# Absolute differences on half an image of one sample at a time, its rows quantised one sample ahead and loaded one unit ahead

## The chip, the cores and the metric

The kernel runs on one core of a Trainium2 chip. The metric is the device time of one execution in microseconds. Executions of a kernel agreed within 0.4% here, so runs are compared directly. Experiments run beside the kernel before on the same chip. Ratios are computed as the mean time of one kernel's runs over that of the other's of the same rounds, so they are not quite the ratio of the medians quoted beside them.

## The reference

Four layers, each added to its input after a group norm: a recurrence along the diagonals of the image, an "adder" convolution, a spectral layer, and a small convolutional encoder and decoder. The change concerns the second layer. On 16 samples of 32 channels of 128x128 it quantises the normalised input to integers of -127 to 127 and takes, in place of products, absolute differences:

```python
def _adder2d(qx, qw):      # out[n,f,i,j] = -sum_{c,kh,kw} |patch - w|
    ...
    def per_out(wk):
        return -jnp.sum(jnp.abs(pr - wk[None, :, None]), axis=1)
    out = jax.lax.map(jax.checkpoint(per_out), wf)
    ...
x = x + _L1_conv_ref(_gn(x), L1_conv_weight)
```

Both kernels use |q - w| = 2 max(q - w, 0) - q + w. VectorE or ScalarE computes max(q - w, 0) for one tap of a filter, in f16. TensorE sums it over the channels with a matrix of constants. The sums of q ("the sums" below) are matmuls on the quantised rows themselves, and the sum of w is one constant per filter.

## The kernel before

A unit is 32 rows of four samples, with 32 channels x 4 samples on the 128 partitions. There are 16 units. All eight accumulators (PSUM banks) belong to the current unit. A unit's quantised rows are made in SBUF from rows loaded in f32; nothing goes back to memory but the result.

```python
for g in range(NG):
    for ch in range(H // R):                                     # R = 32
        xc = xp.tile([128, R + 2, W], F32, name="xc")
        nc.sync.dma_start(xc[:, off : off + n, :], cb_view(x1, g, lo, n))
        ...                                                      # quantise into qa (padded rows), qb
        acc = [ps.tile([128, 512], F32, name="acc") for _ in range(8)]
        for tap in range(9):                                     # the sums: 288 matmuls
            for k in range(8):
                for j in range(4):
                    nc.tensor.matmul(acc[k][32 * j : 32 * j + 32, :], sel16[:, 8, :],
                                     window(tap)[:, 4 * k : 4 * k + 4, :], start=tap == 0, stop=False)
        for f8 in range(8):
            for tap in range(9):                                 # 288 tiles of 4096 per partition
                for j in range(4):
                    ...                                          # j == 3: ScalarE, else VectorE
                ...                                              # 32 matmuls on the four tiles
        for k in range(8):                                       # the finish
            v = xc[:, 1 + 4 * k : 5 + 4 * k, :].rearrange("p r w -> p (r w)")
            nc.vector.scalar_tensor_tensor(v, acc[k], sumw, v, ALU.subtract, ALU.add)
            nc.vector.bn_stats(stat[:, g, 8 * ch + k, :], v)
        nc.scalar.dma_start(cb_view(x2, g, R * ch, R), xc[:, 1 : R + 1, :])
```

The transfers of a unit address memory as `[[HW, C], [CHW, 4], [1, n]]`: the slowest dimension is the 32 channels.

Of the kernel before, what the change touches and what calls it, by code (L numbers as in the profile page):

```python
# [6 lines left out]
F32 = mybir.dt.float32  # L7
F16 = mybir.dt.float16
# [7 lines left out]
HW = H * W  # L16
CHW = C * HW
NG = 4
# [20 lines left out]
def cb_view(t, g, row0, nrows):  # L39

    return bass.AP(t.tensor, t.offset + g * 4 * CHW + row0 * W, [[HW, C], [CHW, 4], [1, nrows * W]])


# [28 lines left out]
def norm_stats(nc, pool, ps, mv, n, avg, eps):  # L72



    mean = pool.tile([128, n], F32, name="ns_mean")
    nc.vector.tensor_copy(mean, mv[:, :, 0])
    p1 = ps.tile([128, 512], F32, name="ps")
    nc.tensor.matmul(p1[:, :n], avg, mean, start=True, stop=True)
    m = pool.tile([128, n], F32, name="ns_m")  # L80
    nc.vector.tensor_copy(m, p1[:, :n])
    d = pool.tile([128, n], F32, name="ns_d")
    nc.vector.tensor_sub(d, mean, m)
    nc.vector.tensor_mul(d, d, d)
    nc.vector.tensor_add(d, d, mv[:, :, 1])
    p2 = ps.tile([128, 512], F32, name="ps")
    nc.tensor.matmul(p2[:, :n], avg, d, start=True, stop=True)
    v = pool.tile([128, n], F32, name="ns_v")
    nc.vector.tensor_copy(v, p2[:, :n])
    return m, inv_sqrt(nc, pool, v, n, eps)  # L90
# [10 lines left out]
def stage0(nc, tc, keep, cst, x, w0, b1, b2, x1):  # L101
# [3 lines left out]
    with ExitStack() as ctx:  # L105
# [104 lines left out]
        with tc.tile_pool(name="s0_ps2", bufs=2, space=PSUM) as ps:  # L210
            out = []
            for v in norm_stats(nc, sm, ps, mv, NG, cst["avg2_bc"], 1e-5):
                p = ps.tile([128, 512], F32, name="ps")
                nc.tensor.matmul(p[:, :NG], cst["bc_to_cb"], v, start=True, stop=True)
                out.append(keep.tile([128, NG], F32, name=f"s0_out{len(out)}"))
                nc.vector.tensor_copy(out[-1], p[:, :NG])
            return out


def stage1(nc, tc, keep, cst, sel16, m1, r1, x1, w, x2):  # L220
# [4 lines left out]
    R = 32  # L225
    with ExitStack() as ctx:
        sm = ctx.enter_context(tc.tile_pool(name="s1_sm", bufs=1))
        r128 = sm.tile([128, NG], F32, name="r128")
        nc.vector.tensor_scalar(r128, r1, 128.0, None, ALU.mult)


        qw = sm.tile([128, 288], F32, name="qw")
        nc.sync.dma_start(qw, bass.AP(w.tensor, w.offset, [[288, 32], [0, 4], [1, 288]]))
        top = sm.tile([128, 1], F32, name="top")
        nc.vector.tensor_reduce(top, qw, AX.X, ALU.max, apply_absolute_value=True)
        alltop = sm.tile([128, 1], F32, name="alltop")
        nc.gpsimd.partition_all_reduce(alltop, top, 128, bass_isa.ReduceOp.max)
        scale = sm.tile([128, 1], F32, name="scale")
        nc.vector.tensor_scalar(scale, alltop, 1.0 / 127.0, 1e-8, ALU.mult, ALU.max)
        nc.vector.tensor_scalar(scale, scale, 2.0**0.5, None, ALU.mult)  # L240
        nc.vector.tensor_scalar(scale.bitcast(I32), scale.bitcast(I32), 0x7F800000, None, ALU.bitwise_and)
        nc.vector.reciprocal(scale, scale)
        nc.vector.tensor_scalar(qw, qw, scale, -127.0, ALU.mult, ALU.max)
        nc.vector.tensor_scalar(qw, qw, 127.0, RND, ALU.min, ALU.add)
        nc.vector.tensor_scalar(qw, qw, RND, None, ALU.subtract)
        neg = sm.tile([128, 288], F32, name="neg")
        nc.vector.tensor_scalar(neg, qw, -1.0, None, ALU.mult)


        taps = sm.tile([128, 32], F32, name="taps")  # L250
        nc.vector.tensor_reduce(taps, qw.rearrange("p (f t) -> p f t", t=9), AX.X, ALU.add)
        tapb = sm.tile([128, 32, 4], F32, name="tapb")
        nc.vector.tensor_tensor(tapb, bcast(taps[:, :], 2, 4), bcast(cst["m4_cb"], 1, 32), ALU.mult)
        sumw = sm.tile([128, 1], F32, name="sumw")
        with tc.tile_pool(name="s1_ps0", bufs=1, space=PSUM) as ps:
            p = ps.tile([128, 512], F32, name="ps")
            nc.tensor.matmul(p[:, :1], tapb.rearrange("p f b -> p (f b)"), cst["ones"][:, :1], start=True, stop=True)
            nc.vector.tensor_scalar(sumw, p[:, :1], 2.0**-7, None, ALU.mult)

        stat = sm.tile([128, NG, 32, 6], F32, name="stat2")  # L260
        xp = ctx.enter_context(tc.tile_pool(name="s1_x", bufs=2))
        tp = ctx.enter_context(tc.tile_pool(name="s1_t", bufs=1))
        qp = ctx.enter_context(tc.tile_pool(name="s1_q", bufs=2))
        dp = ctx.enter_context(tc.tile_pool(name="s1_d", bufs=2))
        with tc.tile_pool(name="s1_ps", bufs=8, space=PSUM) as ps:
            for g in range(NG):
                for ch in range(H // R):
                    lo, hi = max(R * ch - 1, 0), min(R * ch + R + 1, H)
                    off = lo - (R * ch - 1)
                    n = hi - lo  # L270
                    xc = xp.tile([128, R + 2, W], F32, name="xc")
                    nc.sync.dma_start(xc[:, off : off + n, :], cb_view(x1, g, lo, n))


                    qa = qp.tile([128, R + 2, W + 2], F16, name="qa")
                    qb = qp.tile([128, R + 2, W], F16, name="qb")
                    t = tp.tile([128, R + 2, W], F32, name="t")
                    tv, qv = t[:, off : off + n, :], qb[:, off : off + n, :]
                    nc.vector.tensor_scalar(
                        tv, xc[:, off : off + n, :], m1[:, g : g + 1], r128[:, g : g + 1], ALU.subtract, ALU.mult  # L280
                    )
                    nc.vector.tensor_scalar(tv, tv, -127.0, 127.0, ALU.max, ALU.min)
                    nc.vector.tensor_scalar(qv, tv, RND, RND, ALU.add, ALU.subtract)
                    nc.scalar.copy(qa[:, off : off + n, 1 : W + 1], qv)
                    nc.gpsimd.memset(qa[:, :, 0], 0.0)
                    nc.gpsimd.memset(qa[:, :, W + 1], 0.0)
                    for edge, row in ((ch == 0, 0), (ch == H // R - 1, R + 1)):
                        if edge:
                            nc.gpsimd.memset(qa[:, row, :], 0.0)
                            nc.gpsimd.memset(qb[:, row, :], 0.0)  # L290

                    def window(tap):
                        kh, kw = tap // 3, tap % 3
                        return qb[:, kh : kh + R, :] if kw == 1 else qa[:, kh : kh + R, kw : kw + W]

                    acc = [ps.tile([128, 512], F32, name="acc") for _ in range(8)]
                    for tap in range(9):
                        for k in range(8):
                            for j in range(4):
                                nc.tensor.matmul(  # L300
                                    acc[k][32 * j : 32 * j + 32, :],
                                    sel16[:, 8, :],
                                    window(tap)[:, 4 * k : 4 * k + 4, :],
                                    start=tap == 0,
                                    stop=False,
                                )
                    for f8 in range(8):
                        for tap in range(9):
                            ds = []
                            for j in range(4):  # L310
                                i = 9 * (8 * j + f8) + tap
                                if j == 3:
                                    d = dp.tile([128, R, W], F16, name="d_act", bufs=2)
                                    nc.scalar.activation(d, window(tap), AF.Relu, bias=neg[:, i : i + 1])  # L314
                                else:
                                    d = dp.tile([128, R, W], F16, name="d_dve", bufs=6)
                                    nc.vector.tensor_scalar(  # L317
                                        d, window(tap), qw[:, i : i + 1], 0.0, ALU.subtract, ALU.max
                                    )
                                ds.append(d)  # L320
                            for k in range(8):
                                for j in range(4):
                                    nc.tensor.matmul(  # L323
                                        acc[k][32 * j : 32 * j + 32, :],
                                        sel16[:, f8, :],
                                        ds[j][:, 4 * k : 4 * k + 4, :],
                                        start=False,
                                        stop=f8 == 7 and tap == 8,
                                    )
                    for k in range(8):  # L330
# [830 lines left out]
```

## Time and profile before

| | us |
|---|---|
| median of 3 executions | 9256.16 |
| stage, first VectorE tile to end of the last finish | 4524.4 (1432.0 to 5956.4) |
| unit to unit | 283.4 |
| VectorE tile / ScalarE tile, start to start | 1.196 / 3.60 |

The prediction below shows the slices, the chain and the groups. One view it does not show is worth having first: a stretch in which two loads of 2.1 MB ran (columns: the stretch, its length, busy time and instructions of each engine, the granted clock, the mean busy share of the 16 DMA engines, GB/s).

```profile
core 0: us, PE busy (x) PEld busy (x) DVE busy (x) ACT busy (x) POOL busy (x), PEclk, DMA share, GB/s
1412.00:1418.00 6.00, 0.26 (x2) 0.29 (x2) 3.03 (x11) 0.00 (x0) 0.71 (x3) 0.50 0.99 358
```

A share of 0.99 means that these loads used all 16 engines: in the packet records, 16 of their rows move at once in most of this stretch. The 8.32 us of the first of them is the figure that the prediction took for the changed kernel's transfers.

### The profile page before, as it was taken

What the parts mean: (1) busy time and instruction counts of PE and PEld (TensorE: products, weight loads), DVE (VectorE), ACT (ScalarE), POOL (GpSimd) and SP (SyncE); (2) the same over time, 40 slices, a digit from 0 to 9 for tenths busy, and PEclk for the clock granted to TensorE, in tenths of its full rate; (3) what the DMA queues carried; (4) which work ended last, traced back from release to release, by engine and by line L of the source; (5) the groups of instructions that cost most, each with busy time, mean ns of one, the idle gap of its engine ahead of it and who ended that gap; (6) DMA issues with size and microseconds to landing.
All of it is one profiled execution on the core that took longest, in us unless ns stands there. A gap on an engine that the chain in (4) does not pass through costs nothing.

```text
span 9251.5 us, 253991 instructions
## 1 busy us (share of the span) xinstructions
PE 7875.1 (85%) x117746; PEld 5052.1 (55%) x117746; DVE 6114.6 (66%) x7543; ACT 5084.6 (55%) x3270; POOL 332.4 (4%) x529
## 2 busy tenths in 40 slices
PE   4999988999999999999999999794845968768955
PEld 3888874445444444544445544493734645545832
DVE  5444448999999999999999999830634233232233
ACT  1444437989989899998989989700000110101122
POOL 0111110000000000000000000000000000000000
PEclk9999998999999999999999999855555968778977
DMA  9799921000000000000000000242731111111067
GB/s 199 57 80 78 73 28 30 20 20 20 1 20 20 20 20 12 10 20 20 20 20 1 20 20 10 74 126 54 253 107 53 42 57 36 52 42 36 26 161 182
DMA packets 1503138, 494.74 MB, mean 53 GB/s; under 512 B 1416956, under 2 KB 1420540, under 8 KB 1486332
## 3 DMA queue, kind: packets, MB, share of 16 engines
q1 hardware_dynamic: 1460764, 365.54, 24.5%
q10 hardware_dynamic: 41312, 112.95, 3.7%
q8 instruction: 922, 15.11, 0.7%
q14 instruction: 140, 1.15, 0.0%
HBM read 331.12 MB, written 147.33 MB: 52 GB/s over the span
## 4 chain that ended last, share of the span: by engine, by line
DVE 41%; PE 38%; issue 15%; DMA 2%; SPq 2%; ACT 1%; DVEq 0%; ACTq 0%; POOL 0%; POOLq 0%
DVE d_dve L317 35%; PE acc L905 10%; PE pg L179 5%; PE pg L180 4%; PE acc L646 4%; PE acc L565 3%; PE pg L181 2%; PE acc L300 2%; PE p L379 2%; PE acc L793 2%; PE pf L479 1%; DVE xc L332 1%; PE acc L323 1%; DVE stat L333 1%; PE pa L459 1%
## 5 line engine op out<-in xcount | busy, mean ns | idle before, releaser
L323 PE MATMUL acc<-d_dve,sel 128*32 128x512 f16 x27648 | 3994.7, 379 | 43.7 <-DVE d_dve L317 43.3
L323 PEld LDWEIGHTS <-sel 128*32 128x32 f16 x36864 | 2057.5, 95 | 2042.1 <-issue 217.6
L314 ACT ACTIVATE d_act<-qa,neg 128x4096 f16<-128x4096 f16 x768 | 2803.3, 3697 | 131.4 <-PE acc L323 130.3
L317 DVE TENSOR_SCALAR d_dve<-qa,qw 128x4096 f16<-128x4096 f16 x2304 | 2788.5, 1279 | 110.6 <-PE acc L323 86.0
L323 PE MATMUL acc<-d_act,sel 128*32 128x512 f16 x9216 | 2181.2, 380 | 0.0
L314 ACT ACTIVATE d_act<-qb,neg 128x4096 f16<-128x4096 f16 x384 | 1419.4, 3696 | 0.0
L317 DVE TENSOR_SCALAR d_dve<-qb,qw 128x4096 f16<-128x4096 f16 x1152 | 1409.5, 1279 | 0.0
L905 PE MATMUL acc<-xp,fo_all 32*32 32x512 f32 x25600 | 934.9, 625 | 55.4 <-DVE pooled L806 48.8
L905 PEld LDWEIGHTS acc<-xp,fo_all 32*32 32x32 f32 x25600 | 658.4, 105 | 321.6 <-issue 161.6
L179 PE MATMUL pg<-h,bd 128*128 128x256 f32 x2048 | 652.2, 401 | 58.7 <-DVE h L199 58.4
L190 ACT ACTIVATE gt<-pg,bias 128x256 f32<-128x256 f32 x1024 | 400.9, 474 | 546.0 <-PE pg L181 545.8
L180 PE MATMUL pg<-h,bd 128*128 128x256 f32 x2048 | 622.8, 386 | 0.0
L817 ACT ACTIVATE y<-pooled,fo_b 32x128 f32<-32x128 f32 x256 | 102.4, 400 | 843.6 <-DVE pooled L806 840.2
L646 PE MATMUL acc<-xp 32*32 32x108 f32 x16384 | 326.1, 376 | 233.4 <-issue 228.3
L933 DVE TENSOR_TENSOR acc<-acc,cut 128x4 f32<-128x4 f32 x256 | 28.8, 166 | 700.4 <-PE acc L905 699.3
L181 PE MATMUL pg<-xn,bd 128*128 128x2 f32 (+62 forms) x2048 | 425.8, 289 | 9.4 <-DVE xn L163 9.4
L181 PEld LDWEIGHTS pg<-xn,bd 128*128 128x128 f32 x2048 | 396.6, 194 | 66.4 <-DVE xn L163 10.2
L180 PEld LDWEIGHTS pg<-h,bd 128*128 128x128 f32 x2048 | 398.2, 194 | 56.9
L646 PEld LDWEIGHTS acc<-xp 32*32 32x32 f32 x16384 | 257.3, 135 | 302.4 <-issue 282.6
L617 DVE TENSOR_SCALAR xp<-xp,stats 128x2560 f32<-128x2560 f32 (+1 forms) x64 | 101.0, 1579 | 461.5 <-DMA xp<-x_d 461.4
L194 DVE TENSOR_TENSOR c<-c,gt 128x256 f32<-128x256 f32 x256 | 108.4, 424 | 450.0 <-ACT gt L190 450.0
L179 PEld LDWEIGHTS pg<-h,bd 128*128 128x128 f32 x2048 | 341.4, 195 | 65.6 <-issue 50.0
(233 smaller groups left out, 5197.9 us busy)
## 6 DMA issues: line engine op xcount, KB each, us to landing
xr<-x_d SPq DMA_DIRECT2D x64, 1024.0 KB
xp<-x_d SPq DMA_DIRECT2D x48, 1280.0 KB
x_in<-in_x_dram SPq DMA_DIRECT2D x16, 2048.0 KB
res<-in_x_dram SPq DMA_DIRECT2D x32, 1024.0 KB
x_d<-res SPq DMA_DIRECT2D x32, 1024.0 KB
x_d<-xc ACTq DMA_DIRECT2D x16, 2048.0 KB
x_d<-xr ACTq DMA_DIRECT2D x32, 1024.0 KB
out_dram<-xr ACTq DMA_DIRECT2D x32, 1024.0 KB
```

The source lines that it names most:

```text
L179: nc.tensor.matmul(pg[:, q], wmat(0, q), h_in[:, :, 1:], start=True, stop=False)
L180: nc.tensor.matmul(pg[:, q], wmat(1, q), h_in[:, :, :H], start=False, stop=False)
L181: nc.tensor.matmul(pg[:, q, :, : t + 1], wmat(2, q), xn[:, 2 * c : 2 * c + 2, j, : t + 1], start=False, stop=True,)
L190: nc.scalar.activation(gt[:, q], pg[:, q], AF.Tanh if q == 3 else AF.Sigmoid, bias=bias[:, q : q + 1])
L300: nc.tensor.matmul(acc[k][32 * j : 32 * j + 32, :], sel16[:, 8, :], window(tap)[:, 4 * k : 4 * k + 4, :], start=tap == 0, stop=False,)
L314: nc.scalar.activation(d, window(tap), AF.Relu, bias=neg[:, i : i + 1])
L317: nc.vector.tensor_scalar(d, window(tap), qw[:, i : i + 1], 0.0, ALU.subtract, ALU.max)
L323: nc.tensor.matmul(acc[k][32 * j : 32 * j + 32, :], sel16[:, f8, :], ds[j][:, 4 * k : 4 * k + 4, :], start=False, stop=f8 == 7 and tap == 8,)
L379: nc.tensor.matmul(p1[:, i, :], xh[:, 16 * half + i, :], cst["cas"], start=True, stop=True)
L565: nc.tensor.matmul(acc[blk][32 * j : 32 * j + 32, : rows * n], self.w[part, par, tap, :], src[part, top : top + rows, left : left + n], st ...
L646: nc.tensor.matmul(gram[blk][32 * j : 32 * j + 32, at : at + 36 * n], xp[rows, l, 2 + 32 * j : 34 + 32 * j], xp[rows, l : l + n, 32 * j : ...
L905: nc.tensor.matmul(acc[blk][32 * j : 32 * j + 32, :], wf["all"][rows, tap, :], xp[rows, 4 * j + kh : 4 * j + kh + 4, kw : kw + W], start=t ...
```

## The change

Its intent: larger tiles (8192 or 8320 per partition, so half as many instructions), half an image of one sample per unit (64 rows, 32 units), and two sets of four accumulators, so that a unit's finish and the next unit's matmuls no longer wait for each other. The partitions hold four copies of the 32 channels, and a tile serves four filters. To have the copies, the quantised rows go to memory (`q_d`) and are loaded back four times over. Quantising is done one sample ahead, this load one unit ahead. Cut to its core:

```diff
+def jc_rows(t, b, half, n=16 * W):
+    return bass.AP(t.tensor, t.offset + b * CHW + half * 64 * W, [[16 * W, 4], [HW, C], [1, n]])
 ...
+        def quantise(b, half):
+            t = xp.tile([128, 16 * W], F32, name="xq")                    # 2 buffers
+            nc.sync.dma_start(t, jc_rows(x1, b, half))
+            nc.scalar.activation(t, t, AF.Identity, bias=shift[:, b : b + 1], scale=r128[:, b : b + 1])
+            ...                                                          # two VectorE passes into qt
+            nc.sync.dma_start(bass.AP(q_d.tensor, first, [[16 * P, 4], [(H + 2) * P, C], [1, 16 * P]]), flat)
+        def loaded(b, half):
+            q = qp.tile([128, R + 2, P], F16, name="q")                   # 2 buffers
+            nc.sync.dma_start(q, bass.AP(q_d.tensor, first, [[0, 4], [(H + 2) * P, C], [1, (R + 2) * P]]))
+            xr = rp.tile([128, 16 * W], F32, name="xr1")                  # 2 buffers
+            nc.sync.dma_start(xr, jc_rows(x1, b, half))
+            return q, xr
 ...
+                q, xr = following
+                if (b, half) != (B - 1, 1):
+                    following = loaded(b + half, 1 - half)
+                acc = [ps.tile([128, 512], F32, name="acc") for _ in range(4)]
+                ...                                                      # the sums: 144 matmuls, 32x32 tiles
+                for i in range(72):
+                    act = i % 4 == 3
+                    d = dp.tile([128, R, P], F16, name="d_act" if act else "d_dve", bufs=2 if act else 4)
+                    ...                                                  # one tile, then its 16 matmuls
+                    if i == 7 and before:
+                        finish(*before)                                  # ends with the store of xr to x2
+                    if i in (10, 30) and half == 0 and b + 1 < B:
+                        quantise(b + 1, int(i == 30))
```

Statistics and constants are laid out to match, and the other layers keep their work.

## The prediction

> **What bounds the kernel now.** I read first the slices, to place the stage that the change rewrites:
>
> ```profile
> PE   4999988999999999999999999794845968768955
> DVE  5444448999999999999999999830634233232233
> ACT  1444437989989899998989989700000110101122
> PEclk9999998999999999999999999855555968778977
> DMA  9799921000000000000000000242731111111067
> ```
>
> Slices 7 to 26 (231 us each) are the absolute-difference stage. PE, VectorE and ScalarE all show nine tenths there, DMA nothing. So the limit is one of three engines, or their coupling. The chain of waits, by line, decides between them:
>
> ```profile
> DVE d_dve L317 35%; PE acc L905 10%; PE pg L179 5%; PE pg L180 4%; PE acc L646 4%; PE acc L565 3%; PE pg L181 2%; PE acc L300 2%; PE p L379 2%; PE acc L793 2%; PE pf L479 1%; DVE xc L332 1%; PE acc L323 1%; DVE stat L333 1%; PE pa L459 1%
> ```
>
> VectorE's difference tiles carry 35% of the span, the matmuls that consume them (L323) 1%. PE only looks full[...]. Next the costliest groups:
>
> ```profile
> L323 PE MATMUL acc<-d_dve,sel 128*32 128x512 f16 x27648 | 3994.7, 379 | 43.7 <-DVE d_dve L317 43.3
> L314 ACT ACTIVATE d_act<-qa,neg 128x4096 f16<-128x4096 f16 x768 | 2803.3, 3697 | 131.4 <-PE acc L323 130.3
> L317 DVE TENSOR_SCALAR d_dve<-qa,qw 128x4096 f16<-128x4096 f16 x2304 | 2788.5, 1279 | 110.6 <-PE acc L323 86.0
> L317 DVE TENSOR_SCALAR d_dve<-qb,qw 128x4096 f16<-128x4096 f16 x1152 | 1409.5, 1279 | 0.0
> ```
>
> VectorE idles 110.6 us before its 3,456 tiles, ScalarE 131.4 us before its 1,152: in 4.5 ms both are saturated. A tile's recorded duration (1279 ns) is not its price, because neighbours overlap. The price is start to start, from the timeline early in a unit (unit: one pass of the loop, 16 in all):
>
> ```profile
> 2018.02 7.26 DVE L317 TENSOR_SCALAR d_dve<-qa,qw 128x4096 f16<-128x4096 f16 x6 [3.25 <-PE acc L323]
> 2025.20 3.67 DVE L317 TENSOR_SCALAR d_dve<-qb,qw 128x4096 f16<-128x4096 f16 x3
> 2028.79 7.26 DVE L317 TENSOR_SCALAR d_dve<-qa,qw 128x4096 f16<-128x4096 f16 x6
> ...
> 2018.42 7.31 ACT L314 ACTIVATE d_act<-qa,neg 128x4096 f16<-128x4096 f16 x2
> 2025.63 3.69 ACT L314 ACTIVATE d_act<-qb,neg 128x4096 f16<-128x4096 f16 x1
> 2029.23 7.30 ACT L314 ACTIVATE d_act<-qa,neg 128x4096 f16<-128x4096 f16 x2
> ```
>
> Nine VectorE tiles in 10.77 us: 1.196 us each. Three ScalarE tiles in 10.81 us: 3.60 us. A set of four tiles (three and one) takes 3.59 us on either engine, so the split is balanced to a hundredth. What comes on top is at the unit's edge:
>
> ```profile
> 2272.78 1.40 DVE L332 SCALAR_TENSOR_TENSOR xc<-acc,sumw,xc 128x512 f32<-128x512 f32 x2
> 2274.10 1.27 DVE L333 BATCH_NORM_STATS2 stat<-xc 128x6 f32<-128x512 f32 x2
> 2281.72 0.53 ACTq L334 DMA_DIRECT2D x_d<-xc  x1
> 2293.21 7.31 ACT L314 ACTIVATE d_act<-qa,neg 128x4096 f16<-128x4096 f16 x2 [15.45 <-PE acc L323]
> 2300.43 3.69 ACT L314 ACTIVATE d_act<-qb,neg 128x4096 f16<-128x4096 f16 x1
> ```
>
> The finish (eight pairs of L332 and L333) runs 2272.78 to 2282.80, 10.0 us; ScalarE stands 15.45 us meanwhile. Unit spacing from the chain in order of time: L300 pieces begin at 1430.80 and, fourteen units on, at 5398.88, so 283.4 us. The sum agrees: 216 tiles x 1.196 = 258.3, finish 10.0, quantising 2.52 + 2.39 + 2.4 = 7.3, idle 110.6/16 = 6.9; together 282.5.
>
> [...] Tiles read from `qa`, whose rows lie 130 apart, cost the same 1279 ns as those from `qb`, which are contiguous; a padded output is not shown. [...] in the timeline one column's matmuls come every 0.21 us, so 53.6 ns each.
>
> **The change, part by part.** The arithmetic stays: 16 units of 288 tiles of 4096 become 32 units of 72 tiles of 8192. Four copies of the 32 channels fill the partitions, so one tile serves four filters of one sample. Every fourth tile still goes to ScalarE. I cost one new unit.
>
> (1) VectorE tiles: 54. [...] those with kw = 1 compute all 130 columns[...], a third of them. Mean 2274, so 122.8 us. Two units: 245.6 against 258.3.
>
> (2) ScalarE tiles: 18, [...] mean 7049: 126.9 us. The gain is half the fixed parts; the padding takes a little back.
>
> (3) Finish: four pairs in place of eight per unit, 5.0 us, the same total. But it moves to tile 7 of the next unit, and with 4 accumulators of 8 per unit PE can start the next one at once. Before, all eight banks were held, PE waited, and ScalarE stood 15.45 us.
>
> (4) Quantising: before, three f32 passes, 7.3 us of VectorE per unit, and a copy on ScalarE of about 3.8 (not in its 72 tiles). After, twice per sample: [...] Per sample 3.7 and 4.0.
>
> (5) Matmuls: per tile 16 x 53.6 ns = 0.86 us, while a tile arrives every 1.82 (131/72). The sum of the quantised rows: 288 matmuls took about 18 us (18.29 on the chain for 259); now 144 per unit on 32x32 tiles, at most 144 x 53.6 = 7.7 us. Four VectorE buffers hold 9.1 us of work, which covers that.
>
> (6) DMA: a 2.2 MB load per unit, which four copies of the channels cost, and 0.5 MB out per half. A 2.1 MB load took 8.32 us before; a unit is 131 us long. Hidden. At the start the rows now go to DRAM and back before the first tile: about 6 us more.
>
> Sum per sample: VectorE 245.6 + 10.0 + 3.7 = 259.3; ScalarE 253.8 + 4.0 = 257.8. Against 283.4. VectorE is the bound, ScalarE nearly so. For coupling I allow 3 us a sample: VectorE's finish puts it 5 us behind, ScalarE can be a bit under one 7 us tile ahead (two buffers), and regains 0.23 us per set, so most is absorbed. That is a judgement. Stage: 16 x 259.3 = 4149 + 48 = 4197, against 4524 from the first VectorE tile (1432.0) to the end of the finish (5956.4). Less 327, plus 6: a gain of 321, so **8935 us**. The later stages and the recurrence keep their instructions.
>
> **Rivals.** (A) No absorption: every lump on VectorE and ScalarE is exposed, because PE takes tiles in order and the buffers are short. Then a sample is 253.8 + 4.0 + 10.0 + 3.7 = 271.5, gain 16 x 11.9 = 190: about 9066. For it: two buffers of 7 us on ScalarE, and before the 15.45 us wait at each edge. Against: that wait came from held banks, which are now free.
> (B) A DMA takes the place of the wait: the residual rows `xr1` have two buffers but three units in flight, so that load waits for the store after the finish; if the quantiser's load queued behind it, ScalarE and VectorE would stand perhaps 15 us a sample (an estimate from 8.32 us for 2.1 MB, three transfers of 1 MB). That is 240 us back, about 9175. For it: one queue. Against: in the trace quantising of a unit runs one unit ahead of its place in the source (its first pass at 2007.49, just after the previous unit began at 1998), so order follows readiness.
> (C) [...] a tile becomes 4.4 us and the kernel about 3.5 ms slower. Against: equal times for `qa` and `qb`[...].
> (D) PE becomes the bound: even at half clock 1.72 us per tile are under 1.82; little effect expected.
>
> **Range and chances.** No coupling loss at all gives 8887; a small error in the fixed parts (10 ns on 54 x 32 tiles is 17 us) could take it to 8860. Half to two thirds of rival A's loss gives about 9050. So 8860 to 9050. "Faster by over 2%" means under 9071: A alone just reaches it, B and C miss. I give 0.87 faster, 0.10 within 2%, 0.03 slower (C).
>
> **What would show it.** Right: VectorE tiles 2.26 us start to start, ScalarE 7.01, units 131 us apart, VectorE's idle time in the stage under 60 us, PE's waits now for d tiles after nearly each of them, and ScalarE's 15 us gaps gone. Wrong: VectorE waiting for PE where PE waits for ScalarE's tile (A); waits for DMA loads or by the quantiser ahead of VectorE and ScalarE (B); L317's successor at 4.4 us (C); the sum matmuls on the chain for more than 9 us per unit (D).

The prices of the tiles and passes in parts (1), (2) and (4), and rival C's 4.4 us, are estimates of mine: in the trace of the kernel before, all difference tiles have one size, 4096.

## The result, and the profile after

| | before | after |
|---|---|---|
| median, us | 9252.76 (4 runs: the three above and one more) | 9769.06 (4 runs) |
| ratio, 95% interval | 1 | 1.0557 (1.0538 to 1.0575) |
| first VectorE tile of the stage at, us | 1432.0 | 1509.4 |
| stage to the end of the last finish, us | 4524.4 | 4976.0 (1509.4 to 6485.4) |
| VectorE idle before its tiles, us | 110.6 | 849.9 |

The kernel became 5.6% slower, where 3.5% faster was forecast. The slices of the kernel after show how:

```profile
PE   4999963555545554545454555668565776869965
DVE  5444426889878887878787978972253323332233
ACT  1444326889877887879787978950000010101122
DMA  9899831111111111110111111034462111111157
```

In the stage (slices 7 to 27) VectorE and ScalarE no longer stand at nine, but mostly at seven and eight tenths in turn. No engine is full any more, so something is waited for. The chain of waits by line, in the kernel after:

```profile
PE acc L946 9%; DMA q<-q_d 9%; ACT d_act L357 8%; PE pg L174 4%; PE pg L175 4%; DMA x_d<-xr 4%; PE acc L687 3%; DMA xq<-x_d 3%; DVE d_dve L359 3%; PE pg L176 2%; PE acc L606 2%; PE p L420 2%; PE acc L834 1%; PE pf L520 1%; PE acc L364 1%
```

Three transfers of the stage, absent before, now carry about 15% of the span (8.5, 3.6 and 3.2% before rounding): the load of the quantised rows, the store of the result, and the load for the quantiser. The costliest groups after:

```profile
L359 DVE TENSOR_SCALAR d_dve<-q,qw 128x8192 f16<-128x8192 f16 (+1 forms) x1728 | 3940.9, 2359 | 849.9 <-PE acc L364 826.6
L357 ACT ACTIVATE d_act<-q,neg 128x8192 f16<-128x8192 f16 (+1 forms) x576 | 4066.6, 7148 | 602.9 <-PE acc L364 578.0
L341 PE MATMUL acc<-q,sel 32*32 32x512 f16 x4608 | 149.2, 504 | 841.8 <-DMA q<-q_d 841.8
```

Read them from the bottom. PE stands 841.8 us before the sums (L341), waiting for the load (91.2 us of it before the first unit). VectorE's 826.6 and ScalarE's 578.0 us of waiting for PE are the echo of it: their buffers stay full while PE stands. The tiles themselves cost what was predicted. Now one unit's edge in order of time, PE only:

```profile
3214.49 1.05 PE L364 MATMUL acc<-d_act,sel 128*32 128x512 f16 x16 [3.37 <-ACT d_act L357]
3215.35 2.79 PE L364 MATMUL acc<-d_dve,sel 128*32 128x512 f16 x48
3221.62 1.06 PE L364 MATMUL acc<-d_act,sel 128*32 128x512 f16 x16 [3.47 <-ACT d_act L357]
3246.19 2.35 PE L341 MATMUL acc<-q,sel 32*32 32x512 f16 x67 [23.51 <-DMA q<-q_d]
3248.47 1.84 PE L364 MATMUL acc<-d_dve,sel 128*32 128x512 f16 x16
3250.25 0.43 PE L341 MATMUL acc<-q,sel 32*32 32x512 f16 x16
3250.61 1.05 PE L364 MATMUL acc<-d_dve,sel 128*32 128x512 f16 x16
```

The sums do not stand at the unit's start, as the source has them: they are among the matmuls of the *current* unit's tiles. They belong to the *next* unit. The order of PE's instructions in the built program says so (S: sums, D: matmuls on tiles, 16 per tile; first two units):

```
144 S, 144 D, 1 S, 16 D, 16 S, 48 D, 16 S, 16 D, 16 S, 48 D, 16 S, 16 D, ... 3 S, 832 D, ...
```

After nine tiles of unit 0, the sums of unit 1 are spread between tiles 10 and 28; in the trace, the later sums begin after 7 or 8 tiles of the unit before theirs and end after 13 or 17. I take it that the builder's scheduler places work where its inputs should be ready by its own estimate of times; no run shows how it decides. The trace has PE keep to this order: it stands 23.51 us before the sums, and the current unit's next matmuls come only after them, at 3248.47. So a sum whose rows are not there stops the current unit too. The load is issued at 3207.45, when the previous unit's buffer comes free (next view), and lands at 3246.05: it has the first eight tiles of a unit (about 15 us) for its time, not a whole unit. The issuing queue around the same place:

```profile
3030.97 0.50 SPq L313 DMA_DIRECT2D q<-q_d  x1
3045.31 0.54 SPq L323 DMA_DIRECT2D x_d<-xr  x1
3080.99 0.51 SPq L315 DMA_DIRECT2D xr<-x_d  x1
3081.59 0.50 SPq L295 DMA_DIRECT2D xq<-x_d  x1
3082.15 0.54 SPq L306 DMA_DIRECT2D q_d<-qt  x1
...
3207.45 0.51 SPq L313 DMA_DIRECT2D q<-q_d  x1
```

The quantiser's load (L295, 3081.59) stands in the one queue behind the residual load (L315), which waits for a buffer that the store (L323, 3045.31) frees. The chain in order of time has the two transfers end to end, and ScalarE's quantising after them:

```profile
3045.31 35.62 DMA x_d<-xr
...
3081.59 32.04 DMA xq<-x_d
```

That is rival B, for 1 MB transfers that take 35.6 and 32.0 us here. Not all of this is their own: in the packet records of this trace the first row of the store issued at 3045.31 moves at 3067.83, when the load of the quantised rows issued at 3030.97 is nearly through. The store stands 22.5 us behind that load and moves its own rows in 12.7. Why the load takes so long is in the stretches within it (same columns as before):

```profile
3033.00:3044.00 11.00, 7.16 (x108) 3.32 (x101) 11.00 (x9) 11.00 (x2) 0.00 (x0) 0.90 0.26 58
3046.00:3068.00 22.00, 0.89 (x11) 0.00 (x0) 11.30 (x7) 13.11 (x2) 0.00 (x0) 0.50 0.25 60
```

A share of 0.25 is 4 of 16 engines, and 58 to 60 GB/s are a sixth of the 358 before. The packet records say the same: in these two stretches four rows move at once, where it was 16 before. What differs between the two loads is the slowest dimension of their access patterns. Before, the two sides had 32 channels and 128 partitions: 16 engines, share 0.99. In the change every pattern on the memory side begins with a dimension of 4: 4 engines, share 0.25. That the slowest dimension sets the number of engines is my reading of these two cases, and the experiments test it. The prediction did not look at it.

**Theory after this view.** The stage's transfers run on 4 of 16 engines. Their length is exposed in two places: PE's place for the sums, and the one queue ahead of the quantiser. Rivals: the transfers are slow for another reason (rows read four times over, alignment, one in flight), or the loss is in-order coupling with short buffers (rival A), and fast transfers would not bring it back.

### The profile page after: what moved, and what is told of

The parts are those of the page before. It is cut to its first block, busy times and chain, and to the rows that moved or that the text cites. A ratio compares the mean times of both kernels' runs of the same rounds, so it can differ in the third digit from the quotient of the medians.

```text
span 9766.2 us, 249603 instructions
## 1 busy us (share of the span) xinstructions
PE 6187.8 (63%) x117740; PEld 4024.5 (41%) x117740; DVE 5853.4 (60%) x5842; ACT 5005.7 (51%) x2710; POOL 268.6 (3%) x483
## 4 chain that ended last, share of the span: by engine, by line
PE 35%; issue 29%; DMA 17%; ACT 9%; DVE 8%; SPq 1%; another core or an unknown queue 0%; ACTq 0%; POOL 0%; DVEq 0%; POOLq 0%
PE acc L946 9%; DMA q<-q_d 9%; ACT d_act L357 8%; PE pg L174 4%; PE pg L175 4%; DMA x_d<-xr 4%; PE acc L687 3%; DMA xq<-x_d 3%; DVE d_dve L359 3%; PE pg L176 2%; PE acc L606 2%; PE p L420 2%; PE acc L834 1%; PE pf L520 1%; PE acc L364 1%
## 5 line engine op out<-in xcount | busy, mean ns | idle before, releaser
L359 DVE TENSOR_SCALAR d_dve<-q,qw 128x8192 f16<-128x8192 f16 (+1 forms) x1728 | 3940.9, 2359 | 849.9 <-PE acc L364 826.6
L357 ACT ACTIVATE d_act<-q,neg 128x8192 f16<-128x8192 f16 (+1 forms) x576 | 4066.6, 7148 | 602.9 <-PE acc L364 578.0
L364 PE MATMUL acc<-d_dve,sel 128*32 128x512 f16 x27648 | 1928.8, 412 | 704.1 <-DVE d_dve L359 699.8
L364 PEld LDWEIGHTS <-sel 128*32 128x32 f16 x36864 | 1122.6, 103 | 2930.5 <-issue 2290.9
L364 PE MATMUL acc<-d_act,sel 128*32 128x512 f16 x9216 | 706.8, 432 | 870.4 <-ACT d_act L357 868.9
L341 PE MATMUL acc<-q,sel 32*32 32x512 f16 x4608 | 149.2, 504 | 841.8 <-DMA q<-q_d 841.8
L341 PEld LDWEIGHTS <-sel 32*32 32x32 f16 x4608 | 53.6, 93 | 955.3 <-issue 860.6
```

Source lines behind the costliest of these rows:

```text
L341: nc.tensor.matmul(acc[k][32 * j : 32 * j + 32, :], sel16[rows, 8, :], q[rows, row : row + 4, kw : kw + W], start=tap == 0, stop=False,)
L357: nc.scalar.activation(dst, src, AF.Relu, bias=neg[:, i : i + 1])
L359: nc.vector.tensor_scalar(dst, src, qw[:, i : i + 1], 0.0, ALU.subtract, ALU.max)
L364: nc.tensor.matmul(acc[k][32 * j : 32 * j + 32, :], sel16[:, f8, :], d[:, row : row + 4, c : c + W], start=False, stop=i == 71,)
```

## The experiments

All gave correct results. The builder re-plans the order of instructions for each kernel, so even a small edit may move others; the views are checked for it.

### 1. All transfers cut by partition block

```diff
-            nc.sync.dma_start(q, bass.AP(q_d.tensor, first, [[0, 4], [(H + 2) * P, C], [1, (R + 2) * P]]))
+            for j in range(4):
+                nc.sync.dma_start(
+                    q[32 * j : 32 * j + 32], bass.AP(q_d.tensor, first, [[(H + 2) * P, C], [1, (R + 2) * P]])
+                )
```

and the same for `xq`, `xr`, the store to `x2` and the store to `q_d`. Only the slowest dimension becomes 32.

> The changed kernel with each of its stage transfers (rows in for quantising, quantised rows out, quantised rows in, residual in, result out) cut into four by partition block, so that each piece has 32 as its slowest dimension on both sides and not 4. Nothing else changes. Theory (a transfer whose slowest dimension on the memory side is 4 runs on 4 of the 16 DMA engines, 0.25 share in the trace; its 38 us then stands on PE's and ScalarE's streams): DMA share during the load over 0.8, the 2.1 MB load lands in about 10 us in place of 38, units come every 131 us, VectorE's idle time before its tiles falls from 850 to under 100 us, total 8950 (8900 to 9050). Rival 1 (the transfers are slow because the same rows are read four times, or for other traffic on memory): loads still take over 30 us, total within 2% of 9769. Rival 2 (in-order coupling with two ScalarE buffers is the loss): loads are fast but VectorE and ScalarE still wait over 15 us per unit on PE, total over 9400.

Measured: 8896.22 us, ratio to the kernel before 0.9616 (0.96 to 0.9632). A stretch of the load, the two groups, and VectorE in the unit's middle, of this experiment:

```profile
3013.00:3020.00 7.00, 3.82 (x68) 1.86 (x64) 7.00 (x4) 7.00 (x2) 0.00 (x0) 1.00 1.05 223
```

```profile
L372 ACT ACTIVATE d_act<-q,neg 128x8192 f16<-128x8192 f16 (+1 forms) x576 | 4065.6, 7149 | 49.3 <-PE acc L379 31.0
L374 DVE TENSOR_SCALAR d_dve<-q,qw 128x8192 f16<-128x8192 f16 (+1 forms) x1728 | 3937.8, 2359 | 28.6 <-DMA q<-q_d 16.2
```

```profile
3049.13 22.82 DVE L374 TENSOR_SCALAR d_dve<-q,qw 128x8192 f16<-128x8192 f16 x10 [2.15 <-PE acc L379]
3071.86 1.22 DVE L308 TENSOR_SCALAR qt<-xq 128x2048 f16<-128x2048 f32 x1
```

With 32 as the slowest dimension all 16 engines work (a share of 1.05: packets overlap a little), VectorE's idle time is 28.6 us in place of 849.9, and ten of its tiles take 22.73 us start to start, 2.273 each. The load takes 11.4 us from first packet to last. PE's sums stand where they stood, after 7 or 8 tiles, so the gain does not come from a new order there. Rivals 1 and 2 fall. The total was missed by little: it lies under the expected 8900 to 9050. The stage takes 4159.9 us (1453.3 to 5613.2) and the kernel is faster than both.

### 2. Control: the load cut into four by columns

```diff
+            n = (R + 2) * P // 4
+            for j in range(4):
+                nc.sync.dma_start(flat[:, n * j : n * j + n],
+                    bass.AP(q_d.tensor, first + n * j, [[0, 4], [(H + 2) * P, C], [1, n]]))
```

> Control: the load of the quantised rows alone is cut into four transfers too, but by columns, so that each still has 4 as its slowest dimension on the memory side. Same number of transfers as a cut by partition block. Theory (engines by slowest dimension): DMA share stays 0.25, no gain, 9769 within 1%. Rival 3 (several smaller transfers in flight are faster in themselves): the loads get faster and the total falls by 300 us or more.

Measured: 9209.47 us, ratio 0.9956 (0.9936 to 0.9976). My expectation of no gain fell: 560 us less than the changed kernel. Two stretches within loads, of this experiment:

```profile
3128.00:3138.00 10.00, 6.48 (x88) 2.70 (x81) 10.00 (x7) 10.00 (x2) 0.00 (x0) 0.83 0.26 96
3140.00:3150.00 10.00, 1.19 (x14) 0.20 (x7) 10.00 (x8) 10.00 (x2) 0.00 (x0) 0.58 0.26 104
```

Still four engines (0.26), with 4 still the slowest dimension, but together they move 96 to 104 GB/s in place of 60. The trace's records of single packets (one per row and piece) say more: the 17160-byte rows took 1267 ns in the median (13.5 bytes per ns), the 4290-byte pieces 167 ns (25.7). Rows of 17408 bytes in the kernel before took 648 ns (26.9). So there are two causes of the slow load, a factor of four and one of about two, and I had seen one.

### 3. and 4. Half of the cut each

The load of the quantised rows alone cut by partition block, and all others alone.

> Only the load of the quantised rows is cut by partition block; the 1 MB transfers stay on four engines. Theory: PE's wait for the load before the sums (842 us in all) nearly goes, the store, residual load and quantiser load that follow one another on the one queue stay at 27 to 35 us each, and ScalarE's wait for the quantiser's rows (268 us in 12 waits) stays or grows. Total about 9150 (9050 to 9350). Rival 1: no change, 9769.

> The reverse: the 1 MB and 0.5 MB transfers are cut by partition block, the load of the quantised rows stays on four engines. Theory: ScalarE's wait for the quantiser's rows goes (268 us), PE's wait of 20 to 25 us per unit for the quantised rows stays, total about 9500 (9400 to 9650). If the gains of the two halves add up, their sum is the gain of cutting all.

Measured: 8959.6 us, ratio 0.9686 (0.9667 to 0.9705), for the load alone; 9495.6, ratio 1.0265 (1.0245 to 1.0286), for the others. The load alone brings back 809 of the 873 us between the changed kernel and experiment 1 (9769.06 to 8896.22), the others alone 273. They do not add up (1082): each wait hides part of the other. The expectation for the load alone was too cautious, because I thought that ScalarE's wait for the quantiser's rows would stay. It went too (one wait of 53.1 us is left, at the start). The queue of experiment 3:

```profile
3057.15 1.70 SPq L314 DMA_DIRECT2D q<-q_d  x4
3071.63 0.54 SPq L326 DMA_DIRECT2D x_d<-xr  x1
3080.77 0.55 SPq L295 DMA_DIRECT2D xq<-x_d  x1
3087.76 0.54 SPq L318 DMA_DIRECT2D xr<-x_d  x1
```

Two things changed here. The store no longer stands behind a 38 us load: 9.1 us after it is issued (3071.63) the queue goes on (3080.77), where the changed kernel needed 35.7 (3045.31 to 3080.99). And the builder put the quantiser's load before the residual load. No run separates the two. In experiment 4, with 9495.6 us within its expected range, PE still waits 796.9 us for the load.

### 5. The sums after the tiles of their own unit

```diff
-                for tap in range(9):    # the sums, before the tiles, start=tap == 0
 ...
-                                start=False, stop=i == 71,
+                                start=i == 0, stop=False,
 ...
+                for tap in range(9):    # the same 144 matmuls here, start=False, stop=tap == 8
                 before = b, half, acc, xr
```

> The changed kernel with the sums of the quantised rows issued after the 72 tiles of their own unit instead of before them (the first tile's matmuls now start the accumulation). The transfers stay as they are, on four engines at 38 us. In the program of the changed kernel the scheduler had moved the next unit's 144 sums among tiles 9 to 20 of the current unit, so that PE, taking its instructions in order, waits there for a load that was only issued at the unit's start. Theory: it is this place in PE's order that exposes the load; with the sums late the load has a whole unit (131 us) and PE's wait for it (842 us) goes, with VectorE's for PE (827 us). Total 9000 to 9300. Rival (slow transfers hold the stage up wherever PE needs them, through the one queue): still over 9500.

Measured: 9526.77 us, ratio 1.0292 (1.0269 to 1.0315): over 9500, as the rival had it. The waits in the stage of this experiment (who waited for whom, us in total, times, longest):

```profile
PE acc L351 <- ACT d_act L344: 1238.3, 278, 53.2
PE acc L351 <- DVE d_dve L346: 923.0, 842, 94.7
ACT xq L296 <- DMA xq<-x_d: 599.9, 24, 47.6
DVE d_dve L346 <- PE acc L351: 594.4, 65, 50.6
```

PE's wait for the load, 841.8 us, is gone (no such line but for the first unit), as the theory said. But ScalarE's wait for the quantiser's rows grew to 599.9 us in the one queue, and it holds PE and VectorE in its turn. One wait took the place of the other. This run alone does not decide.

### 6. Three buffers for the quantised rows

```diff
-        qp = ctx.enter_context(tc.tile_pool(name="s1_q", bufs=2))
+        qp = ctx.enter_context(tc.tile_pool(name="s1_q", bufs=3))
```

> The changed kernel with three buffers for the quantised rows in place of two, PE's order as in the changed kernel (sums hoisted). Theory: the load for the next unit no longer waits for the previous unit's buffer, so it can be issued a unit earlier and is there when PE comes to the hoisted sums: PE's wait for the load nearly goes, total 9000 to 9300. Rival (the rate of the four engines is the limit, as 5.7 MB per sample pass through them): under 150 us gained.

Measured: 9170.69 us, ratio 0.9907 (0.9888 to 0.9927), in the expected range. PE's order in the trace is the changed kernel's, matmul for matmul in this stage, and the transfers are still on four engines, but the load is issued a unit earlier. Its waits:

```profile
ACT xq L296 <- DMA xq<-x_d: 230.7, 12, 22.3
DVE d_dve L359 <- PE acc L364: 211.2, 37, 28.7
PE acc L341 <- DMA q<-q_d: 95.5, 2, 92.9
```

PE waits for the load in two places only, 92.9 of the 95.5 us before the first unit. What is left is 230.7 us in 12 waits for the quantiser's rows. So the four engines' rate as such is not the limit. (The 5.7 MB of the expectation are what passes per unit, by the sizes of the five transfers, not per sample.)

### 7. Late sums with the small transfers cut

The edit of experiment 5 with the cut of `xq`, `xr` and both stores; the load stays on four engines.

> Late sums, as before, and the 1 MB and 0.5 MB transfers cut by partition block; the load of the quantised rows is left at 38 us on four engines. With the transfers slow, late sums had taken away PE's wait for the load, but ScalarE's wait for the quantiser's rows had grown from 268 to 600 us behind the one queue. Theory (PE's place for the sums exposes the load, the one queue exposes the rest): with both mended a 38 us load is hidden in a unit, total 8960 (8880 to 9080). Rival (a load of 38 us cannot be hidden): over 9300.

Measured: 8917.77 us, ratio 0.963 (0.9602 to 0.9658). The load still takes 37 us, and nothing waits for it after the first unit. The two groups of this experiment:

```profile
L356 ACT ACTIVATE d_act<-q,neg 128x8192 f16<-128x8192 f16 (+1 forms) x576 | 4067.9, 7156 | 65.4 <-DMA q<-q_d 47.8
L358 DVE TENSOR_SCALAR d_dve<-q,qw 128x8192 f16<-128x8192 f16 (+1 forms) x1728 | 3934.8, 2361 | 45.9 <-DMA q<-q_d 45.7
```

This decides what experiment 5 left open: a 37 us load is hidden once PE does not come to it early and the queue ahead of the quantiser is short. Alone the two edits had brought 242 and 273 us; together they bring 851. Both places were needed.

### 8. to 10. Why a long row runs at half the rate

Three edits to the load of the changed kernel: channels of `q_d` 33856 bytes apart in place of 33800, so that each row starts at a multiple of 64 bytes; the same load described as four-byte elements (`.bitcast(F32)` on both sides); and two column pieces of 8580 bytes in place of four of 4290.

> The changed kernel with the channels of the quantised copy in memory 33856 bytes apart in place of 33800, so that every row of the load starts at a multiple of 64 bytes; nothing else. The cut by columns had shown 17160-byte rows at 1267 ns each and quarter rows at 167 ns (668 for four) on the same four engines. Theory X (alignment of the long rows halves their rate): rows take about 650 to 720 ns, the load 21 to 24 us, total near the cut by columns, 9200 (9150 to 9300). Theory Y (length, or one transfer in flight at a time, is what halves the rate): rows stay at about 1270 ns, total 9769 within 1%.

> The changed kernel with the load of the quantised rows described as 4290 four-byte elements a row in place of 8580 two-byte ones: the same 17160 bytes, the same four engines, one transfer. Rows of 17408 bytes described as four-byte elements took 648 ns before, these take 1267. Theory (the element type of the description is what halves the rate of a long row): rows near 650 ns, load 20 to 24 us, total near the cut by columns, 9200 (9150 to 9300). Rival (it is something else in these rows, such as their number or the memory they lie in): rows stay at 1270 ns, total 9769 within 1%.

> The changed kernel with the load of the quantised rows cut by columns into two transfers of 8580-byte rows, still on four engines. On four engines rows of 17160 bytes took 1267 ns each (13.5 bytes per ns) and quarter rows of 4290 bytes 167 ns (25.7); neither the start's alignment nor the element type changed that. If the length of a row sets it, half rows show on which side 8580 lies: 334 ns each and a load of about 24 us (total near 9210) where they are short enough, or 630 ns and 37 us (total near 9769) where they are not. If the rate falls gradually with length, something between, about 480 ns, 30 us and 9450.

Measured: 9781.5 us, ratio 1.0567 (1.0546 to 1.0588), with rows still at 1268 ns; 9766.62, ratio 1.0547 (1.0516 to 1.0577), rows 1267 ns; and 9382.4, ratio 1.0124 (1.0095 to 1.0154). Neither alignment to 64 bytes nor the element type is the cause. Half rows fall into two kinds, 327 ns (26.2 bytes per ns) in the median and 541 ns or more in the slowest quarter, and the load takes 28.2 us. So in this load, the shorter the pieces, the fewer run at half rate. But the kernel before moved rows of 17408 bytes at full rate, and experiment 3, with several long-row transfers in flight, had 1339 ns a row.

The traces say one thing more: the slow rows come first. In the changed kernel the first eighth of a load's rows takes 1307 ns in the median and the last 1050; of the half rows, the first eighth takes 629 and the last 325. No run shows why. Experiment 1 did not cure it: its rows still took 1339 ns, and its 8192-byte rows, in pieces of 32 partitions on 16 engines, 600 ns where four engines had taken 311. What makes these rows slow stays open.

For the time it is a matter of size. From 37.8 us (packets, first to last, median of 32 loads) to 28.2, 23.6 and 11.5 the kernel goes from 9769 to 9382, 9209 and 8960. Reckoned from the changed kernel each time, that is 1.3, 1.2 and 0.96 us per us of load in 32 units. In the first two ScalarE's wait for the quantiser's rows fell too, from 268 to 155 and 156 us.

### 11. Cut by partition block, with the padded distance

> All transfers cut by partition block and the padded distance between channels together. The stage is bound by VectorE and ScalarE once the transfers are hidden, so nothing more is to be had than cutting alone gave: 8896 within 0.5%, whether or not alignment changes the rate of a row.

Measured: 8895.78 us, ratio 0.9612 (0.9596 to 0.9628), as expected: with the transfers hidden there is nothing more to be had from them. The kernel of experiment 1 is as good and is the simpler one.

## Why the prediction was wrong, point by point

- **Parts (1), (2) and (4), the prices: right.** VectorE's tile was put at 2274 ns and took 2273 in experiment 1; two tiles of 4096 had taken 2392. ScalarE's was put at 7049 ns. In the trace of experiment 1, 14 tiles are busy 98.84 us without a gap, 7.06 us each; two of 4096 had taken 7.20. The traces now show a part of the price that does not grow with the tile. Recorded tiles of 4096 (before) and 8192 (after) take 1279 and 2348 ns on VectorE, 3697 and 7112 on ScalarE. That is 0.261 and 0.834 ns per element, which leaves about 127 ns of the 1196 start to start, and 185 of the 3600. Quantising was put at 1.20 and 0.67 us on VectorE and 1.99 on ScalarE; the recorded durations are 1.22, 0.70 and 2.08. Rival C, that output rows 130 apart slow VectorE's tiles, did not happen: tiles of 8192 elements, written with such rows, are recorded at 2348 ns, those of 8320, written without gaps, at 2381. Its 4.4 us are near the pace of an f32 pass before, 4224 elements in 2.36 us at the fastest (L282), at which 8192 would take 4.6.
- **The sum of the stage: right once the transfers are hidden.** Experiment 1 needs 4159.9 us where 4197 was put, 260.0 per sample against a bound of 259.3. The 3 us allowed for coupling were hardly used, so rival A fell. Its total of 8896 lies within 40 us of the forecast 8935.
- **Part (6) is the step that failed: "A 2.1 MB load took 8.32 us before; a unit is 131 us long. Hidden."** Two things in it were wrong. The duration was taken from a load with another access pattern. With 4 as its slowest dimension the new load ran on four engines (share 0.25), and its long rows at half rate besides (1267 ns for 17160 bytes, where 17408 had taken 648): 38 us. And "a unit is 131 us long" supposed the load had a unit's time. It had seven or eight tiles, about 15 us, because the sums of the next unit had been moved there.
- **Part (3), "PE can start the next one at once", was half of the story.** The next unit's sums did move forward, and so made PE's in-order stream depend on a load that had only just been issued. "Order follows readiness", which I used against rival B, seems to be the mechanism here: ready by the builder's estimate, not by the clock. Part (3) and rival A also misread the edge of the kernel before. There PE's matmuls waited 10.2 us in all for the finish, 1.08 at the edge shown; while ScalarE stood, PE was at the sums, from 2273.57 to 2291.1. And such waits were 9 in all (130.3 us), not one at each edge.
- **Rival B was the right mechanism for the quantiser's load, and its sum was luck.** I gave it 15 us a sample, 240 in all, from transfers at the old rate; ScalarE waited 268 us, and cutting the small transfers alone was worth 273. But the store and the load took 35.6 and 32.0 us, most of the store's behind the load of the quantised rows, which rival B did not have in the queue. Nor did it cover the larger part, PE's wait for the quantised rows, worth 809 us when its load alone was cut.
- **The start.** It was put at 6 us more. The first VectorE tile came 77 us later (1509.4 against 1432.0), and 21 us later in experiment 1: the way through memory and back is three transfers in series (the quantiser's load, the store to `q_d`, the load from it).
- The forecast of what would show it wrong held: waits for loads by the quantiser and ahead of VectorE and ScalarE. Rival D did not occur; 67 sums took 2.35 us, 35 ns each. Its doubling at half clock is in the trace: the 16 matmuls on a tile take 1.84 us where the granted clock is 0.50 (at 3248.47), and 1.05 where it is 0.99 (at 3250.61).

## What to carry to other kernels

A transfer's time is read from a transfer with the same access pattern, not from one with the same bytes: look at the slowest dimension on both sides before taking a rate over (here 4 on the memory side went with a share of 0.25 to 0.26, 32 with 0.99 and 1.05), and at the DMA share in the stretch afterwards (0.25 is four engines). A load that is "one unit ahead" in the source has only the time between its buffer's release and the first instruction *in an in-order stream* that needs it (here about 15 us, not a unit), so check the built order of the consumer. When one of two waits in series is removed, the other may take its place (here 841.8 us of PE's wait went, and ScalarE's grew from 268 to 599.9), and a test that removes one alone can look like a refutation.
